# Where the sums of the experts are added to the output, and up to which step expert work is dealt out

## The chip, the cores and the metric

The kernel runs on one core of a Trainium2 chip. The metric is the device time of one execution in microseconds (us); less is better. Three runs of the kernel before gave 1726.62, 1738.76 and 1740.42 us, with a median of 1738.76. A separate execution was taken with the hardware profiler.

## The reference, cut to what matters

Eight sequences (batches) of 512 tokens with 256 features go through two layers. The first is a two-directional state space block plus a mixture of experts. The second, which the change touches, is an attention block plus another mixture of experts, both on the same normalized input:

```
xn = layernorm(x)
x = x + attention(xn) + experts(xn)
```

The attention has 16 heads of 16 features and all 512 x 512 scores of a batch, which are scaled by a decay band before the softmax; its output goes through one more projection, Wo. The experts are seven two-matrix networks (256 to 1024 to 256, with relu) on at most 512 tokens each, chosen by the router's two largest weights, and an eighth that hands the token through with a weight. In the kernel that last weight is noop. An expert's results are added to the rows of the tokens that it was given, so one token's row can get sums from two experts.

## The kernel before, in words

The second layer is one loop of 128 steps: 8 batches by 4 groups of four heads (g) by 4 blocks of 128 keys (c). In step n, TensorE makes four score tiles of 128 x 512 (s_ps, L1576); VectorE multiplies each by the decay band and takes its maximum (L1579); ScalarE takes exponentials of the step before (L1593); TensorE multiplies those of the step before that with the values (o_ps, L1601). Four such products accumulate a group.

**A group's division.** divide() runs a little in each step after a group's last block. It writes the group's sums to HBM (od, L1693). After every second group it loads the row sums of eight heads (sm, L1703) and their numerators, turned, into one half of oT (L1708). VectorE inverts sm (L1711); SP writes the inverse out (rd, L1712) and loads it back spread over all rows (rb, L1714). VectorE multiplies oT by rb (L1717). Two halves make oT complete. oT has one buffer, so the first half of the next batch can only be loaded when the last reader of the one before is done. That reader is finish(): for each of four token blocks, TensorE multiplies by Wo (fin, L1536), ScalarE copies (fo), and VectorE adds noop times the token's own row (L1540), into x_sb, which has a place for all eight batches. The last batch goes another way, without HBM: its first eight heads are turned on chip by first_heads() (tq, tb), the last eight by Ending, which also projects and writes the output (L1530).

**The experts** are a generator of 238 turns, WORK. Two turns make one pair of the first matrix's columns or half of an output tile; each turn is about a microsecond of TensorE. In each step, fill() takes up to two turns and a third one if the work is behind its due time, which grows evenly from step 4 to step LAST. A turn can end with an expert output half done; then nothing else is dealt out before the next turn. Each expert output tile (e_yo) is added row by row into x1 in HBM by a scatter that GpSimd issues (L1437). x1 holds the layer's input x. Each of these scatters waits for the landing of the one before.

**soon()** runs one part of what stands first in the list urgent: finish() or first_heads(). It is called once a step ahead of the turns, and does nothing while an expert output is half done. When all turns are spent, fill() calls it as well, up to three times a step in all.

**combine()** starts when all turns are spent. It adds x1 into x_sb, batch by batch, by accumulating DMAs that GpSimd issues (L1548), the last batch first, and then writes seven batches from x_sb to the output (L1557). The last batch is written by Ending.

Order matters as follows. The engines take their instructions strictly in program order, and so does each queue of DMAs. SP's queue carries the loads of queries, keys and values (qT, kT, vt), the expert weights (e_w, 1 MB each) and all DMAs of divide(). GpSimd's queue (q0) carries the gathers and scatters of the experts and the accumulating DMAs. At the end of the program a flag is loaded by all engines (L1880) and a branch is taken; only behind that does GpSimd wait for its DMAs to land.

Of the kernel before, what the change touches and what calls it, by code (L numbers as in the profile page):

```python
# [12 lines left out]
ALU = mybir.AluOpType  # L13
# [5 lines left out]
B, S, DM = 8, 512, 256  # L19
NT = B * S  # L20
NTILE = NT // P
TPB = S // P
# [36 lines left out]
def bc(ap, axis, shape):  # L59

    return ap.unsqueeze(axis).to_broadcast(shape)
# [3 lines left out]
def tile_kernel(ctx: ExitStack, tc: tile.TileContext, t, out: bass.AP):  # L65
    nc = tc.nc
    V, A, G, T, Y = nc.vector, nc.scalar, nc.gpsimd, nc.tensor, nc.sync
# [46 lines left out]
    x1 = dram.tile([NT, DM], FP, name="x1", tag="x1")  # L114
# [7 lines left out]
    def rows_of(src, b):  # L122
        return src[b * S : (b + 1) * S, :].rearrange("(c p) d -> p c d", p=P)
# [248 lines left out]
    def bank(name, shape, tag="gen"):  # L372
        return mp.tile(shape, FP, name=name, tag=("e", "s")[tag] if isinstance(tag, int) else tag, bufs=2)
# [6 lines left out]
    def rows_in():  # L380
# [29 lines left out]
        for u, b0 in zip(us, order[::2]):  # L410
# [9 lines left out]
            nm = r0p.tile([P, G2], FP, name="nm", tag="nm")  # L420
            V.scalar_tensor_tensor(nm, mv[:, :, 0], -1.0, rs, ALU.mult, ALU.mult)
            finish(1)
            for i in range(G2):
                A.activation(
# [3 lines left out]
            for k, b in enumerate(both):  # L428
# [5 lines left out]
                for o in range(KC):  # L434
# [7 lines left out]
                    else:  # L442
                        A.copy(xTs[b][:, o, :], tp)
            turned.append((both, halves))
        finish(2)
        return xTs

# [120 lines left out]
    with ExitStack() as es:  # L568
# [26 lines left out]
        held = {}  # L595
# [770 lines left out]
    x_sb = res.tile([P, NTILE, DM], FP, name="x_sb", tag="x_sb")  # L1366
    with tc.tile_pool(name="a1", bufs=1) as p1, tc.tile_pool(name="a2", bufs=2) as p2, tc.tile_pool(
# [109 lines left out]
        def columns(tq):  # L1477

            tq = tq.rearrange("p g (i r) -> p (g i) r", r=32)
            V.tensor_tensor(low[:, :8], low[:, :8], tq[:, :, AD], ALU.min)  # L1480
            sm = p2.tile([P, 8], FP, name="smq", tag="smq")
            V.reciprocal(sm, tq[:, :, AD])
            oq = p2.tile([P, 8, AD], FP, name="oq", tag="oq")
            V.tensor_tensor(oq, tq[:, :, :AD], bc(sm, 2, [P, 8, AD]), ALU.mult)
            return oq.rearrange("p h d -> p (h d)")

        def first_heads(oT, os):

            for c in range(TPB):
                at = slice(c * P, (c + 1) * P)  # L1490
                tq = bank("tq", [P, 2, P])
                for k in range(2):
                    T.transpose(tq[:, k, :], os[k][:, at], ident)
                oq = columns(tq)
                yield
                yield
                tp = bank("tb", [P, P])
                T.transpose(tp, oq, ident)
                A.copy(oT[:, 0, at], tp)
                yield  # L1500

        class Ending:
# [11 lines left out]
            def divide(self):  # L1514
                tq = psum.tile([P, 2, P], FP, name="tq", tag="s_ps", bufs=4)
                T.transpose(tq[:, 0, :], self.os[:, self.at], ident)
                T.transpose(tq[:, 1, :], self.last, ident)
                self.oq = columns(tq)
# [13 lines left out]
        def finish(b, oT):  # L1532
            for c in range(TPB):
                fp = bank("fin", [P, DM])
                for j in range(KC):
                    T.matmul(fp, oT[:, j, c * P : (c + 1) * P], w_o[:, j, :], start=(j == 0), stop=(j == KC - 1))  # L1536
                fo = p2.tile([P, DM], FP, name="fo", tag="fo")
                A.copy(fo, fp)  # L1538
                xi = x_sb[:, b * TPB + c, :]
                V.scalar_tensor_tensor(xi, xi, noop[:, b * TPB + c : b * TPB + c + 1], fo, ALU.mult, ALU.add)  # L1540
                yield
            finished.add(b)

        def combine():


            def add(b):
                G.dma_start(out=x_sb[:, b * TPB : (b + 1) * TPB, :], in_=rows_of(x1, b), accum_op=ALU.add)  # L1548

            for b in (B - 1, *range(B - 2)):  # L1550
                add(b)
            yield
            while B - 2 not in finished:
                yield
            add(B - 2)
            for b in range(B - 1):
                G.dma_start(out=rows_of(out, b), in_=x_sb[:, b * TPB : (b + 1) * TPB, :])  # L1557

        class Step:
            def __init__(self, b, g, c, inputs):
# [117 lines left out]
        def divide(b, g, op, od, rd, held):  # L1680


            if b == B - 1:
                if g == 0:
                    held.append(p1.tile([P, KC, S], FP, name="oT", tag="oT"))
                held.append(p1.tile([P, S], FP, name="ol", tag="ol", bufs=3))
                A.copy(held[-1], op)
                if g == 1:
                    urgent.insert(0, first_heads(held[0], held[1:]))
                return  # L1690
            os = p1.tile([P, S], FP, name="os", tag="row", bufs=2)
            A.copy(os, op)
            Y.dma_start(out=od[g].rearrange("i r s -> (i r) s"), in_=os)  # L1693
            yield
            if g % 2 == 0:
                return
            j = g // 2
            if j == 0:
                held.append(p1.tile([P, KC, S], FP, name="oT", tag="oT"))
            oT = held[0]  # L1700
            sm = p2.tile([P, 32], FP, name="sm", tag="sm")
            for gg in range(2):
                Y.dma_start(  # L1703
                    out=sm[64 * gg : 64 * gg + 64, :],
                    in_=od[2 * j + gg, :, AD, :].rearrange("i (p f) -> i p f", f=32),
                )
            for gg in range(2):
                Y.dma_start(out=oT[64 * gg : 64 * gg + 64, j, :], in_=od[2 * j + gg, :, :AD, :])  # L1708
            yield
            V.tensor_tensor(low, low, sm, ALU.min)  # L1710
            V.reciprocal(sm, sm)  # L1711
            Y.dma_start(out=rd[8 * j : 8 * j + 8, :].rearrange("h (p f) -> (h p) f", f=32), in_=sm)  # L1712
            rb = p1.tile([P, S], FP, name="rb", tag="row", bufs=2)
            Y.dma_start(out=rb, in_=bc(rd[8 * j : 8 * j + 8, :], 1, [8, AD, S]))  # L1714
            yield
            yield
            V.tensor_tensor(oT[:, j, :], oT[:, j, :], rb, ALU.mult)  # L1717
            yield
            if g == 3:
                urgent.insert(0, finish(b, oT))  # L1720

        with tc.manual_schedule(engines=ENGINES):
# [15 lines left out]
            finished = set()  # L1738
            urgent, idle, chains = [], [], []
            WORK = NE1 * 2 * (1 + FC + 2 * 4)  # L1740
            LAST = 118
            spent = 0

            def due():

                return WORK * (n - 4) / (LAST - 4)

            rows, number1 = combine(), None
            e1, e2 = given()
            work = experts()  # L1750
# [44 lines left out]
            for n in range(N + 2):  # L1795

                if n < N:
                    b, g, c = steps[n]
# [40 lines left out]
                if m >= 0:  # L1839
                    s = done[m]  # L1840
                    if s.c == 0:
                        s_op = psum.tile([P, S], FP, name="o_ps", tag="o_ps", bufs=2)
                    s.values(s_op)
                    if s.c == TPB - 1:
                        if m == N - 1:
                            tails = [Ending(s.b, c, s_op, s.scratch[2]) for c in range(TPB)]
                        else:
                            chains.append(divide(s.b, s.g, s_op, *s.scratch))
                            next(chains[-1], None)
# [87 lines left out]
def build(arrays):  # L1937
    import concourse.bacc as bacc

    nc = bacc.Bacc("TRN2", target_bir_lowering=False, num_devices=1)  # L1940
    t = {
        k: nc.dram_tensor(f"in_{k}_dram", v.shape, mybir.dt.from_np(v.dtype), kind="ExternalInput").ap()
        for k, v in arrays.items()
    }
    out = nc.dram_tensor("out_0_dram", (NT, DM), FP, kind="ExternalOutput").ap()
    with tile.TileContext(nc) as tc:
        tile_kernel(tc, t, out)
    return nc
# [10 lines left out]
```

## Time and profile before

| what | us |
|---|---|
| time of the profiled execution | 1731.81 |
| its span | 1730.0 |
| TensorE busy | 1571.1 (91%) |
| VectorE busy | 1172.8 (68%) |
| ScalarE busy | 917.1 (53%) |
| GpSimd busy | 573.1 (33%) |
| attention loop, steps 0 to 127 | about 1170 to 1710 |
| eight accumulating DMAs, issue of the first | 1669.83 |
| last computation (L1879) | 1723.33 |

The chain of work that ended last is TensorE for 73% of the span and VectorE for 17%. Granted clock means the share of full speed that TensorE's clock had. In lists by order of time the first two columns are the start and the duration in us, then come engine, line, operation, output and inputs, and in brackets how long the engine stood idle before and for what. SPq and POOLq are the queues that issue DMAs; "x6" is a count, and the duration of a group reaches from its first start to its last end. A matmul in fp32 stands in the trace as several records, so "x8" are four score tiles or two turns of expert work. Windows list, for each stretch, the busy time of each engine with its count, then granted clock, DMA share and GB/s.

### The profile page before, as it was taken

Reading aid. Unit: us, or ns where it says so; the run is one execution under the profiler, and the core shown is the slowest. Engines: PE = TensorE matmul, PEld = TensorE weight load, DVE = VectorE, ACT = ScalarE, POOL = GpSimd, SP = SyncE. Lnnn points to the kernel's source line nnn. Section 1 sums busy time; section 2 is a strip of 40 time slices with the busy share of each in tenths; the row PEclk is TensorE's granted clock in tenths of the full one; section 3 lists DMA queues with packets and bytes.
Section 4 is the critical chain, followed back from the end, with each engine's and each line's share of the span. In section 5 each row is a group of like instructions: output and inputs, shape, how many; then the busy total and the mean of one; then the engine's idle time right before and its main releaser. Section 6 shows DMA issues by size and latency. Waiting matters only on the chain.

```text
span 1730.0 us, 25735 instructions
## 1 busy us (share of the span) xinstructions
PE 1571.1 (91%) x8700; PEld 963.3 (56%) x8700; DVE 1172.8 (68%) x3067; ACT 917.1 (53%) x2173; POOL 573.1 (33%) x518
## 2 busy tenths in 40 slices
PE   6556799989999999999789898889999999999996
PEld 6324467767777677677445555644445445444442
DVE  6577775576576665775786836547777777777674
ACT  4222345445354454454455643137777777777773
POOL 0031556556564465564532421010111111112030
PEclk7676899999999999999989899669999999999996
DMA  8010346455554564464355624133423343334254
GB/s 298 18 55 0 137 151 221 156 178 177 173 194 157 164 212 158 160 219 159 83 118 166 184 86 136 50 122 118 137 81 107 101 134 102 88 113 136 71 89 134
DMA packets 131821, 231.09 MB, mean 134 GB/s; under 512 B 20109, under 2 KB 93839, under 8 KB 120528
## 3 DMA queue, kind: packets, MB, share of 16 engines
q1 hardware_dynamic: 101952, 119.46, 22.0%
q0 software_dynamic: 28656, 108.69, 20.7%
q8 instruction: 73, 1.20, 0.3%
q10 hardware_dynamic: 1072, 1.18, 0.2%
q14 instruction: 68, 0.56, 0.1%
HBM read 176.75 MB, written 53.58 MB: 133 GB/s over the span
## 4 chain that ended last, share of the span: by engine, by line
PE 73%; DVE 17%; ACT 4%; DMA 3%; issue 2%; POOL 0%; SPq 0%; ACTq 0%; DVEq 0%; POOLq 0%
PE pj L943 8%; PE s_ps L1576 7%; PE o_ps L1601 7%; PE h_ps L640 7%; PE y_ps L664 7%; PE e_hp L1419 5%; PE e_yp L1432 5%; PE op L1088 3%; PE yd L1169 3%; DVE cv L956 3%; PE seg L1131 3%; PE sp L1199 2%; ACT s L1593 2%; PE yoff L1187 2%; DVE s L1579 2%
## 5 line engine op out<-in xcount | busy, mean ns | idle before, releaser
L1579 DVE CUSTOM_DVE_ANT_0 s<-s_ps,band 128x512 f32<-128x512 f32 x512 | 323.3, 687 | 142.5 <-PE s_ps L1576 138.4
L1593 ACT ACTIVATE s<-s,ng 128x512 f32<-128x512 f32 x512 | 325.7, 708 | 0.0
L943 PE MATMUL pj<-xT,w_w_in 128*128 128x512 f32 x384 | 198.1, 642 | 8.9 <-DVE cv L956 6.6
L1437 POOL DMA_INDIRECT x<-e_yo,number x28 | 45.0, 1606 | 432.6 <-ACT e_yo L1436 386.2
L1576 PE MATMUL s_ps<-qT,kT 16*128 16x512 f32 x1024 | 166.4, 671 | 4.4 <-DMA qT<-qd 4.4
L956 DVE SCALAR_TENSOR_TENSOR cv<-pj,w_conv_w,cv 128x511 f32<-128x511 f32 (+2 forms) x192 | 143.4, 747 | 21.9 <-ACT cv L952 17.4
L1115 POOL TENSOR_TENSOR au<-da,half 128x512 f32<-128x512 f32 x64 | 77.9, 1217 | 228.1 <-PE seg L1131 153.1
L640 PEld LDWEIGHTS h_ps<-xdT,w 128*128 128x128 f32 x1152 | 138.1, 193 | 19.3 <-issue 18.6
L1601 PE MATMUL o_ps<-s,wv 128*32 128x512 f32 x1024 | 144.3, 636 | 1.2 <-ACT w L1589 1.2
L640 PE MATMUL h_ps<-xdT,w 128*128 128x128 f32 x1152 | 141.4, 276 | 0.7 <-DMA w<-in_w_dram,w_idx 0.7
L664 PE MATMUL y_ps<-w,hT 128*128 128x256 f32 x576 | 138.7, 385 | 0.0
L664 PEld LDWEIGHTS y_ps<-w,hT 128*128 128x128 f32 x576 | 108.3, 193 | 30.0 <-issue 16.1
L943 PEld LDWEIGHTS pj<-xT,w_w_in 128*128 128x128 f32 x384 | 70.1, 200 | 90.8 <-issue 78.8
L1576 PEld LDWEIGHTS s_ps<-qT,kT 16*128 16x128 f32 x1024 | 51.6, 190 | 120.5 <-DVE w L1586 41.9
L1432 PE MATMUL e_yp<-e_w,e_hT 128*128 128x256 f32 x448 | 114.0, 392 | 1.4 <-ACT e_yo L1436 0.9
L1419 PE MATMUL e_hp<-e_xdT,e_w 128*128 128x256 f32 x448 | 111.9, 388 | 3.5 <-ACT fo L1538 2.2
L1178 DVE TENSOR_TENSOR yT<-yT,yd 128x512 f32<-128x512 f32 (+1 forms) x64 | 43.8, 684 | 104.8 <-PE yd L1169 103.8
L1144 ACT ACTIVATE mt<-seg,mid 64x64 f32<-64x64 f32 x512 | 109.4, 309 | 0.8
L1432 PEld LDWEIGHTS e_yp<-e_w,e_hT 128*128 128x128 f32 x448 | 79.9, 189 | 52.3 <-issue 31.9
L1419 PEld LDWEIGHTS e_hp<-e_xdT,e_w 128*128 128x128 f32 x448 | 81.9, 190 | 39.4 <-ACT s L1593 15.4
L960 ACT ACTIVATE th<-cv 128x512 f32<-128x512 f32 x64 | 40.3, 630 | 116.1 <-DVE cv L956 108.8
L952 ACT ACTIVATE cv<-pj,w_conv_b,w_conv_w 128x512 f32<-128x512 f32 x64 | 49.8, 778 | 95.1 <-PE pj L943 91.0
(341 smaller groups left out, 2827.3 us busy)
## 6 DMA issues: line engine op xcount, KB each, us to landing
ex<-exd SPq DMA_DIRECT2D x96, 128.0 KB
fr<-fdd SPq DMA_DIRECT2D x64, 128.0 KB
e_w<-in_ei_dram SPq DMA_DIRECT2D x7, 1024.0 KB
e_w<-in_eo_dram SPq DMA_DIRECT2D x7, 1024.0 KB
od<-os SPq DMA_DIRECT2D x28, 256.0 KB
vd<-vt SPq DMA_DIRECT2D x16, 272.0 KB
vt<-vd SPq DMA_DIRECT2D x8, 544.0 KB
u<-in_u_dram SPq DMA_DIRECT2D x8, 512.0 KB
```

The source lines that it names most:

```text
L640: T.matmul(hp[:, i, :], w1[:, k * FF + f * P : k * FF + (f + 1) * P], xdT[:, k * P : (k + 1) * P], start=(k == 0), stop=(k == KC - 1),)
L664: T.matmul(yp, hT[f // 4][:, f % 4, :], w2[:, f * DM : (f + 1) * DM], start=(f == 0), stop=(f == FC - 1),)
L943: T.matmul(pj, w_in[:, k, o * P : (o + 1) * P], self.xT[:, k, :], start=(k == 0), stop=(k == KC - 1))
L956: V.scalar_tensor_tensor(cv[:, s:], pj[:, : S - s], conv_w[:, q, 3 - s : 4 - s], cv[:, s:], ALU.mult, ALU.add)
L1115: G.tensor_tensor(self.au, bc(da[:, d, self.i, :], 2, HH), bc(TRI[d], 1, HH), ALU.mult)
L1144: A.activation(mt[lo, over, h], seg[lo, over, h], AF.Exp, bias=mid[lo, self.i, h : h + 1])
L1419: T.matmul(hp, w1[:, k, f * P : (f + 1) * P], xdT[:, k, :], start=(k == 0), stop=(k == KC - 1))
L1432: T.matmul(yp, hT[:, f, c * P : (c + 1) * P], w2[:, f, :], start=(f == 0), stop=(f == FC - 1))
L1576: T.matmul(sp[i], self.k[r, cols], self.q[r, :], start=True, stop=True)
L1579: V.tensor_tensor_reduce(out=self.p[i], in0=sp[i], in1=band[:, at : at + S], scale=1.0, scalar=KEEP, op0=ALU.mult, op1=ALU.max, accum_out= ...
L1593: A.activation(self.p[i], self.p[i], AF.Exp, bias=self.ng[:, i : i + 1])
L1601: T.matmul(op[32 * i : 32 * i + 32, :], self.wv[:, i, :], self.p[i], start=(self.c == 0), stop=(self.c == TPB - 1),)
```

## The change

A batch that is finished is written to the output at once, by SP. Behind the experts the last batch is still added into x_sb; for the seven others x1 is added to the output in HBM, where both the source and the destination lie in HBM. So the seven additions into x_sb and the seven writes by GpSimd are gone, and there are seven writes by SP and seven accumulating DMAs into the output. Each of the latter waits for its batch's write. first_heads() goes to the end of the list urgent, not to its front. LAST is 124, not 118.

```diff
@@ finish(b, oT)
+            Y.dma_start(out=rows_of(out, b), in_=x_sb[:, b * TPB : (b + 1) * TPB, :])
             finished.add(b)
 
         def combine():
-            def add(b):
-                G.dma_start(out=x_sb[:, b * TPB : (b + 1) * TPB, :], in_=rows_of(x1, b), accum_op=ALU.add)
-            for b in (B - 1, *range(B - 2)):
-                add(b)
-            yield
-            while B - 2 not in finished:
-                yield
-            add(B - 2)
-            for b in range(B - 1):
-                G.dma_start(out=rows_of(out, b), in_=x_sb[:, b * TPB : (b + 1) * TPB, :])
+            b = B - 1
+            G.dma_start(out=x_sb[:, b * TPB : (b + 1) * TPB, :], in_=rows_of(x1, b), accum_op=ALU.add)
+            for b in range(B - 1):
+                while b not in finished:
+                    yield
+                G.dma_start(out=rows_of(out, b), in_=rows_of(x1, b), accum_op=ALU.add)
@@ divide
                 if g == 1:
-                    urgent.insert(0, first_heads(held[0], held[1:]))
+                    urgent.append(first_heads(held[0], held[1:]))
@@ the loop's constants
-            LAST = 118
+            LAST = 124
```

Batches and steps are counted from 0. The order in which the changed program's instructions stand on each engine is known without a run.

## The prediction

> **What bounds the kernel now.** I read the stages first (busy time in windows of 50 us), then the chain of waits, then TensorE, SP, DVE and GpSimd in order of time. From 1170 us to the end runs the attention loop of 128 steps. A step with two turns of expert work is the sum of its TensorE work: s_ps 1.07 + expert 1.93 + o_ps 1.00 = 4.00 us in the chain; DVE needs about 3.0 us of it and waits. So the loop is TensorE's, until the experts end in step 118:
>
> ```profile
> 1661.41 1.14 PE L1576 MATMUL s_ps<-qT,kT 16*128 16x512 f32 x8
> 1665.40 1.53 PE L1576 MATMUL s_ps<-qT,kT 16*128 16x512 f32 x8
> ...
> 1684.62 2.09 PE L1576 MATMUL s_ps<-qT,kT 16*128 16x512 f32 x8
> ...
> 1689.34 1.19 PE L1576 MATMUL s_ps<-qT,kT 16*128 16x512 f32 x8
> 1704.82 2.09 PE L1576 MATMUL s_ps<-qT,kT 16*128 16x512 f32 x8
> ```
>
> These are the starts of steps 118, 119, 123, 124 and 127. Behind 119 nothing fills TensorE; transposes of the last batch wait for DVE (first line below, 2.24 us idle), and then the granted clock (third number from the right) falls to a half, as the windows say:
>
> ```profile
> 1682.26 0.33 PE L1498 MATMUL tb<-ident,oq 128*128 128x128 f32 x1 [2.24 <-DVE oq L1484]
> 1680.00:1682.00 2.00, 0.03 (x1) 0.00 (x0) 1.93 (x11) 1.67 (x3) 1.15 (x2) 1.00 1.22 186
> 1684.00:1686.00 2.00, 2.00 (x12) 0.52 (x8) 0.00 (x0) 1.44 (x3) 0.75 (x1) 0.50 1.25 196
> ```
>
> Beside this tail run the accumulating DMAs (GpSimd in order of time):
>
> ```profile
> 1665.39 1.55 POOL L1437 DMA_INDIRECT x<-e_yo,number  x1 [6.57 <-ACT e_yo L1436]
> 1669.83 10.53 POOL L1548 DMA_DIRECT2D x_sb<-x  x8 [2.89 <-DVE x_sb L1540]
> 1679.47 1.68 POOL L1557 DMA_DIRECT2D out_dram<-x_sb  x1
> 1696.01 0.75 POOL L1557 DMA_DIRECT2D out_dram<-x_sb  x1 [1.90 <-DMA x_sb<-x]
> ```
>
> Eight sums of 512 KB move from 1672 to 1693.5, 2.69 us each at 195 GB/s; the writes end at 1703.5. The last computation, L1879, starts at 1723.33; flag load, branch and barrier take the rest to 1730.0. GpSimd waits there for its DMAs at 1724.5, with about 1 us to spare, since TensorE comes to the barrier later: DMAs that land by 1725.5 cost nothing now.
>
> The third place is the single oT buffer, in SP's and DVE's order of time for batch 6:
>
> ```profile
> 1616.44 1.07 SPq L1708 DMA_DIRECT2D oT<-od  x2
> 1617.56 3.28 SPq L1466 DMA_DIRECT2D kT<-kd  x6
> 1621.38 0.34 SPq L1712 DMA_DIRECT2D rd<-sm  x1
> 1623.06 0.61 SPq L1714 DMA_DIRECT2D rb<-rd  x1
> 1629.20 0.68 DVE L1717 TENSOR_TENSOR oT<-oT,rb 128x512 f32<-128x512 f32 x1
> 1351.65 0.69 DVE L1717 TENSOR_TENSOR oT<-oT,rb 128x512 f32<-128x512 f32 x1 [1.97 <-DMA rb<-rd]
> ```
>
> The last line (batch 2) shows that this chain is short of time already: DVE waited 1.97 us for rb. Four of fourteen such products waited, 5.8 us in all.
>
> **1. Dealing to step 124.** The number of expert turns stays the same; in the changed program's instruction order the seven steps with three turns become two-turn steps, and the last turns stand in step 123. Up to step 124 TensorE has, beyond what it had done before step 119, five more bare steps, 5 x 2.07 = 10.35 us, and the four projections of batch 6 (fin, 1.06 us each, now in steps 118 to 122), 4.24 us. 1665.40 + 14.6 = 1680.0, against 1689.34: -9.35 us. That holds if TensorE stays the bound: its sums give 68.5 us a batch, 69.4 are measured.
>
> **2. The tail.** Appending first_heads puts its transposes into steps 124 to 127, where they were in 122 to 124. A transpose (tb) that stands in the same step as its DVE columns stalls the step: before, 6.89 us (step 122) and 6.92 (124); others took 4.72, 3.88, 4.68. Now 124 and 125 stall and 126 does not: 6.3 (like 122, with one pair of transposes less and half of it at full clock) + 6.92 + 4.72 = 17.95 us up to step 127, where 1704.82 - 1689.34 = 15.48 were: +2.5. From step 127 to the end I keep 25.2 us. Parts 1 and 2 make -6.85. Bounds: at full clock (o_ps 1.00 and s_ps 1.07 for 1.87 and 2.06) the three steps are 5.7 + 6.1 + 3.5 = 15.3 us and the end some 2 shorter, -11.5 in all; with 8.0 for step 125 and 6.9 for 124, about -5.
>
> **3. What the slower pace does to oT.** finish() runs one projection at a call of soon(), and none while an expert output is half done. At the new pace more calls fall on half-done outputs: the last fin of batches 3, 4 and 5 moves from steps 74, 90, 106 to 76, 92, 108, the thirteenth of the next batch. oT has one buffer, so L1708 of that batch waits for it, and SP's queue stands: six kT loads (not needed for some steps), then rd and rb, for which DVE waits in L1717 one step on; DVE's own place for L1717 has not moved. With T the start of step 108: fin ends T + 2.13; two oT issues 1.07 and six kT 3.28 make T + 6.5 for rd; rb goes 2.64 us behind (median of the seven such pairs, 1.68 to 3.05), T + 9.1; where DVE waited, rb landed 4.28 to 4.62 us after its issue: T + 13.5. L1717 is due 3.87 us into the next step (1629.20 - 1625.33), which begins at T + 5.06: T + 8.9. DVE stalls 4.6 us; in a quiet step its fourth read of s_ps ends at 1653.12 and the next s_ps (from 1653.42) needs that bank at about 1654.2, a slack of 1.1 us, so TensorE loses 3.5 us, three times: **+10.5**. Lower bound 0 (both landings like the shortest in such a chain, 1.41 us: T + 9.3); upper, with 3.05 and 4.62 and, in batch 5, a 1 MB weight load ahead on SP (2.7 us at the 390 GB/s of the plain writes), about +15. I take the middle because its rows are the same transfers in the same order.
>
> A TensorE gap of about 2 us also comes with each of these waits. The row shows a clock falling after 2.2 us idle, and half clock from 1682.7 to 1689.3, 3.3 us lost; the 1.97 us DVE wait at 1351 left it at 1.00 for its whole 50 us window. I take 0, and keep +3.3 each for the range. [...]
>
> **4. The outputs.** Seven SP writes replace seven GpSimd writes: 0.34 us of SP's issue each, waiting for the DVE result of the last fin. Behind them in SP's queue stand od writes and loads due two or more steps on: 0, at most +2 together if rb queues behind 512 KB (1.3 us).
> Of the eight sums only x_sb of the last batch stays into SBUF and goes first; it is read some 22 us later, so it is hidden. Seven are HBM to HBM, which no row shows. Nearest are the sums into SBUF, 2.69 us for 512 KB, and the scatter-adds into HBM, 128 KB in 1.2 to 1.4 us from first to last packet, where the middle 0.3 us also runs at 184 to 205 GB/s. So 2.69, and 4 x 1.4 = 5.6 as the other end. Before, DMA traffic began 10.6 us behind the start of the last expert step; now that step starts at 1676 + 10.5 = 1686.5, traffic 1697.1, the first sum lands 1699.8, seven more 1718.6. The cover reaches 1725.5 + 3.65 = 1729.2: price **0**, up to 4.2 us a sum; at 5.6 it is 1739.0, +9.8. GpSimd's later wait blocks nothing else.
> [...]
>
> **Sum.** -6.85 + 10.5 = +3.65 us on the profiled execution's 1731.81 (span 1730.0 and 1.81 around it): **1735.5**. The median of the runs shown is 1738.76, of 1726.62 to 1740.42, so executions spread by -5 to +9 about the profiled one.
>
> **The rivals.**
> A, the oT waits are absorbed (rb lands in 1.4 to 2 us): 1725.0, with the clock up in the tail 1720.3. For it: ten of the fourteen products found rb landed. Against: every landing that a wait measures took over 4.2 us, and rd now starts 7 us later than in the rows above. 0.25.
> B, the clock falls at each oT wait: +10, 1745.4. For it the 2.2 us row, against it 1351. 0.15.
> C, slower: the HBM-to-HBM sums take over the end. One price decides, that of a sum; from 4.2 us on it counts, and the time is 1699.8 + 7 x price + 4.5 + 1.81: 1745.3 at 5.6, above 1% at 6.2, 1751.6 at 6.5. [...] 0.15.
> D, nothing moves where I say (the pace does not change the order): excluded, the order is known. The forecast keeps 0.45.
>
> 1% of the median, 17 us, is about what a measurement of this kernel can tell from no change. Forecast, A and half of B and C lie within it: same 0.70. Slower by more: the upper half of C, B joined to long waits, 0.20. Faster by more needs A at full clock and a low draw of the spread: 0.10. The range goes from A at 1722 to the lower part of C, 1752.
>
> **What would show it.** s_ps of step 124 starts 9 us earlier less the waits before it (about 1690); L1717 of batches 4, 5, 6 waits 4 to 6 us for rb, and s_ps two steps on comes 3 to 4 us late; TensorE at half clock from step 124 or 125; q0 traffic from about 1697 to 1719. L1717 without waits makes A, a clock below 1 in steps 78, 94, 110 makes B, q0 traffic beyond 1729 makes C. I am wrong altogether if the 2.07 us of bare steps or the stalls of the last transposes do not hold.

## The result, and the profile after

The changed kernel takes 1759.48 us (median of four executions, 1752.63 to 1761.59); beside it the kernel before takes 1737.24 us. The ratio is 1.0121, 95% interval 1.0072 to 1.0171: slower by about 1.2%, and outside the predicted range of 1722 to 1752. The profiled execution took 1757.68 us, span 1755.8. One execution of e6 below took 1866.47 us at a mean granted clock of 0.81, where all others had 0.91 to 0.94; the ratios leave it out.

TensorE in order of time, as before (start, duration, instruction, idle time ahead of it):

```profile
1679.09 1.14 PE L1569 MATMUL s_ps<-qT,kT 16*128 16x512 f32 x8
...
1707.27 1.14 PE L1569 MATMUL s_ps<-qT,kT 16*128 16x512 f32 x8
...
1711.89 0.30 PE L1498 MATMUL tb<-ident,oq 128*128 128x128 f32 x1 [3.11 <-DVE wv L1590]
1712.12 1.79 PE L1594 MATMUL o_ps<-s,wv 128*32 128x512 f32 x8
1713.84 2.09 PE L1569 MATMUL s_ps<-qT,kT 16*128 16x512 f32 x8
...
1719.41 0.45 PE L1498 MATMUL tb<-ident,oq 128*128 128x128 f32 x1 [2.86 <-DVE oq L1484]
...
1722.08 2.09 PE L1569 MATMUL s_ps<-qT,kT 16*128 16x512 f32 x8
...
1726.80 2.09 PE L1569 MATMUL s_ps<-qT,kT 16*128 16x512 f32 x8
```

The s_ps lines are steps 118, 124, 125, 126 and 127. Step 124 starts at 1707.27, 17.9 us later than before, where about 1690 was forecast; step 118 is 17.7 us late already. So most of the loss lies ahead of the tail. The two tb lines are the stalls of steps 124 and 125.

The third place of the profile before, SP's queue and DVE's product by rb, here in batch 4, with DMAs of batch 5 and the products of batches 5 and 6 behind it:

```profile
1480.18 1.07 SPq L1701 DMA_DIRECT2D oT<-od  x2
1481.30 2.77 SPq L1466 DMA_DIRECT2D kT<-kd  x6
1484.30 0.34 SPq L1705 DMA_DIRECT2D rd<-sm  x1
1487.03 0.61 SPq L1707 DMA_DIRECT2D rb<-rd  x1
1491.48 0.69 DVE L1710 TENSOR_TENSOR oT<-oT,rb 128x512 f32<-128x512 f32 x1 [4.71 <-DMA rb<-rd]
1492.46 1.06 PE L1594 MATMUL o_ps<-s,wv 128*32 128x512 f32 x8 [2.60 <-DVE wv L1590]
...
1554.21 1.07 SPq L1701 DMA_DIRECT2D oT<-od  x2
1555.33 0.46 SPq L1414 DMA_DIRECT2D e_w<-in_eo_dram  x1
1560.54 0.34 SPq L1705 DMA_DIRECT2D rd<-sm  x1
1565.23 0.61 SPq L1707 DMA_DIRECT2D rb<-rd  x1
...
1569.87 0.69 DVE L1710 TENSOR_TENSOR oT<-oT,rb 128x512 f32<-128x512 f32 x1 [9.06 <-issue]
1570.85 1.94 PE L1594 MATMUL o_ps<-s,wv 128*32 128x512 f32 x8 [5.75 <-DVE wv L1590]
...
1645.42 0.69 DVE L1710 TENSOR_TENSOR oT<-oT,rb 128x512 f32<-128x512 f32 x1 [5.24 <-DMA rb<-rd]
1646.40 1.07 PE L1594 MATMUL o_ps<-s,wv 128*32 128x512 f32 x8 [3.13 <-DVE wv L1590]
```

DVE stands 4.71, 9.06 and 5.24 us in front of rb; behind it stands wv, and for wv TensorE stands 2.60, 5.75 and 3.13 us. For the second of these waits the profile names no releaser ("issue" in the row); that it is rb there too is read from its issue, which lies 4.64 us ahead of the product (4.45 and 4.18 us in batches 4 and 6). That chain was forecast, in these three batches. What was not is in the windows around the third of them (length, then busy time of TensorE, weight load, DVE, ScalarE, GpSimd; third from the right TensorE's granted clock, then DMA share and GB/s):

```profile
1644.00:1646.00 2.00, 0.00 (x0) 0.00 (x0) 0.58 (x1) 0.02 (x1) 0.00 (x0) 1.00 1.02 342
1646.00:1648.00 2.00, 1.60 (x10) 0.79 (x12) 2.00 (x7) 0.00 (x0) 0.00 (x0) 0.87 0.93 249
1648.00:1650.00 2.00, 2.00 (x8) 1.02 (x5) 1.61 (x8) 0.99 (x3) 0.00 (x0) 0.50 0.23 42
1652.00:1654.00 2.00, 2.00 (x6) 1.46 (x5) 0.64 (x4) 1.13 (x4) 0.00 (x0) 0.50 0.20 78
```

Each gap is followed by 6.8 to 10.2 us at half clock. The pairs of steps around the three waits (78 and 79, 94 and 95, 110 and 111) took 14.35, 19.20 and 15.20 us for the 7.98 us of two quiet steps: 24.8 us more.

GpSimd and the same view of the end:

```profile
1711.55 1.39 POOL L1548 DMA_DIRECT2D x_sb<-x  x1 [2.87 <-DVE smq L1482]
1712.36 9.52 POOL L1552 DMA_DIRECT2D out_dram<-x  x7
```

```profile
1714.00:1715.00 1.00, 1.00 (x8) 0.35 (x8) 0.00 (x0) 1.00 (x2) 1.00 (x4) 0.50 1.02 125
...
1734.00:1735.00 1.00, 1.00 (x7) 0.20 (x3) 0.00 (x0) 0.41 (x1) 0.00 (x0) 0.50 1.24 199
1735.00:1736.00 1.00, 1.00 (x5) 0.00 (x0) 0.00 (x0) 0.00 (x0) 0.00 (x0) 0.50 1.03 163
```

One sum into SBUF and seven within HBM, 4.2 MB, move from 1714.1 to 1735.8: 2.7 us each, the rate of the sums into SBUF before (2.69 us). The last computation (L1872) starts at 1747.42, so they are hidden.

Where the 25.9 us between the two profiled executions went, from step 7 of the loop, whose start differs by 1.3 us:

| stretch | before | after | difference |
|---|---|---|---|
| step 7 to step 124 | 507.7 | 526.9 | +19.2 |
| step 124 to 127 | 15.48 | 19.53 | +4.05 |
| step 127 to the last computation | 18.5 | 20.6 | +2.1 |
| last computation to the end of the span | 6.7 | 8.4 | +1.7 |

### The profile page after: what moved, and what is told of

Same layout as the page of the kernel before. It is cut to its first block, busy times and chain, and to the rows that moved or that the text cites. A ratio compares the mean times of both kernels' runs of the same rounds, so it can differ in the third digit from the quotient of the medians.

```text
span 1755.8 us, 25758 instructions
## 1 busy us (share of the span) xinstructions
PE 1575.5 (90%) x8700; PEld 963.3 (55%) x8700; DVE 1178.3 (67%) x3067; ACT 917.7 (52%) x2173; POOL 567.5 (32%) x511
## 5 line engine op out<-in xcount | busy, mean ns | idle before, releaser
L640 PEld LDWEIGHTS h_ps<-xdT,w 128*128 128x128 f32 x1152 | 139.9, 195 | 19.3 <-issue 18.5
```

What stands on the lines that cost most here:

```text
L640: T.matmul(hp[:, i, :], w1[:, k * FF + f * P : k * FF + (f + 1) * P], xdT[:, k * P : (k + 1) * P], start=(k == 0), stop=(k == KC - 1),)
```

## The experiments

Executions differ in when the loop's step 7 begins (between 1172 and 1200 us in the profiled runs below, though what lies ahead of the loop is the same code), so besides the median each profile is read from the start of step 7 to the start of the last computation ("loop"). Before it is 541.7 us, after 567.0.

| run | median us | ratio to before | loop us |
|---|---|---|---|
| e1 three halves of oT | 1735.80 | 0.999 [0.9954, 1.0027] | 545.0 |
| e2 pace alone | 1756.21 | 1.0123 [1.0071, 1.0175] | 565.5 |
| e3 outputs alone | 1740.19 | 1.0018 [0.9992, 1.0044] | 547.8 |
| e4 loads behind | 1754.67 | 1.0104 [1.0070, 1.0138] | 559.9 |
| e5 filler | 1754.32 | 1.0114 [1.0057, 1.0170] | 555.7 |
| e6 product two steps later | 1735.94 | 0.9997 [0.9972, 1.0022] | 542.4 |
| e7 tail in turn | 1747.96 | 1.0067 [1.0044, 1.0091] | 559.3 |
| e8 = e6 + e7 | 1727.02 | 0.9947 [0.9922, 0.9972] | 535.4 |
| e9 = e1 + e6 + e7 | 1725.49 | 0.9934 [0.9909, 0.9959] | 524.0 |
| e10 = e9 at step 118 | 1723.66 | 0.9902 [0.9872, 0.9932] | 531.5 |
| e11 = e9, tail filled | 1730.65 | 0.9956 [0.9934, 0.9979] | 531.9 |
| e12 rd ahead of the loads | 1751.40 | 1.0072 [1.0045, 1.0099] | 554.9 |
| e13 = e10 again | 1725.90 | 0.9928 [0.9901, 0.9956] | 531.6 |
| e14 = e9 at step 121 | 1723.19 | 0.9920 [0.9889, 0.9952] | 526.8 |
| e15 = e9 again | 1726.50 | 0.9927 [0.9898, 0.9957] | 525.2 |
| e16 before, tail in turn | 1728.26 | 0.9932 [0.9904, 0.9960] | 530.3 |

**The theory** is that the pace makes the last projections late, the single oT buffer makes SP, rb and DVE late, and TensorE's clock falls in the gap. **Rivals**: the new outputs cost it; the denser expert work slows the loads.

**e1: no wait for the buffer.**

```diff
-            if j == 0:
-                held.append(p1.tile([P, KC, S], FP, name="oT", tag="oT"))
-            oT = held[0]
+            held.append(p1.tile([P, S], FP, name="oT", tag="oT", bufs=3))
+            oT = held[j]
```

(and the users of oT take the half j; to make room the fall-back branch, which does not run here, loads its rows in quarters.)

> oT is held as two halves of 512 columns out of three buffers, so that the load of the next batch's first half finds a free one and does not wait for the last projection. Theory (the wait for the single oT buffer, and the clock that falls behind it): the three pairs of steps at 1486.8, 1560.8 and 1640.2 that took 14.35, 19.20 and 15.20 us go back to 2 x 3.99 = 7.98 us each, 24.8 us less: about 1757.7 - 24.8 = 1733 (ratio to the kernel before 0.99 to 1.00), DVE waits at the product by rb of 2 us or less in batches 4, 5 and 6, TensorE's clock 1.00 there. Rival 1 (the new outputs cost it): unchanged, 1757. Rival 2 (the denser expert work itself slows the loads): rb still comes late, over 1750.

Measured: 1735.80, 22 us back in the loop. Batches 4 and 6 have no wait at the product any more. In batch 5 DVE still waits 4.32 us: as in the changed kernel, a 1 MB expert weight stands right behind the oT load, and rd and rb come behind it; the clock falls there for 6.8 us. Batch 1 keeps a wait of 3.30 us. So the theory holds for batches 4 and 6 in full, and in batch 5 for about half of the wait.

**e2 and e3: the two halves of the change apart.** e2 is the kernel before with

```diff
-                    urgent.insert(0, first_heads(held[0], held[1:]))
+                    urgent.append(first_heads(held[0], held[1:]))
...
-            LAST = 118
+            LAST = 124
```

> The kernel before with the experts dealt to step 124 and first_heads appended, its outputs left as they were (sums into SBUF, then seven writes by GpSimd). Theory (pace alone makes the loss): about as slow as the changed kernel, 1757; at most 5 us more if the seven writes behind the sums end last (sums 1714 to 1736, then 7 x 1.4 us: 1746, about when the last computation starts). Rival 1 (the outputs cost it): about 1737.

and e3 has the diff's other part (finish() writes, combine() adds in memory) without these lines.

> The kernel before with the new outputs alone (SP writes each finished batch, GpSimd adds the experts' sums in memory), dealing to step 118 and the order of first_heads as before. Theory: no change, 1732 to 1741 (ratio 0.998 to 1.002); the sums take 2.69 us each as into SBUF. Rival 1: 1750 or more.

e2 reproduces the whole loss: ratio 1.0123 for 1.0121, with waits at rb of 4.54, 9.02 and 5.33 us in batches 4, 5 and 6. e3's interval holds 1. Its profile, though, shows a cost that the median does not settle. SP in batch 3, and DVE's product:

```profile
1414.29 1.07 SPq L1701 DMA_DIRECT2D oT<-od  x2
1415.46 0.41 SPq L1542 DMA_DIRECT2D out_dram<-x_sb  x1
1415.92 4.12 SPq L1466 DMA_DIRECT2D kT<-kd  x6
1420.20 0.34 SPq L1705 DMA_DIRECT2D rd<-sm  x1
1423.35 0.61 SPq L1707 DMA_DIRECT2D rb<-rd  x1
...
1427.91 0.69 DVE L1710 TENSOR_TENSOR oT<-oT,rb 128x512 f32<-128x512 f32 x1 [4.73 <-DMA rb<-rd]
```

The same place in the kernel before:

```profile
1410.04 1.07 SPq L1708 DMA_DIRECT2D oT<-od  x2
1411.16 2.77 SPq L1466 DMA_DIRECT2D kT<-kd  x6
...
1420.90 0.69 DVE L1717 TENSOR_TENSOR oT<-oT,rb 128x512 f32<-128x512 f32 x1 [1.67 <-DMA rb<-rd]
```

The 512 KB write L1542 stands between oT and the loads; the six loads take 4.12 us of issue where they took 2.77, and DVE waits 4.73 us where it waited 1.67. The clock fell here as well, for 3.4 us; the two steps (62 and 63) took 13.43 us where the same two took 9.81. In the changed kernel the same order stands in batch 1, with a wait of 3.40 us and two steps of 12.11 (e2, without the write, waited 1.53 there, and the two took 8.59). So one of the seven SP writes cost about 3.5 us in each of these two executions; for the others no step up to 123 shows a cost above 0.6 us.

**e4 and e12: rd and rb ahead of the loads.** e4 moved load_some(6) behind the chains in every step; e12 only in the step that issues rd and rb:

```diff
-                load_some(6)
+                if n % 16 != 11:
+                    load_some(6)
                 for chain in list(chains):
                     if next(chain, "end") == "end":
                         chains.remove(chain)
+                if n % 16 == 11:
+                    load_some(6)
```

> The changed kernel with the step's six q and k loads issued behind the chains' DMAs instead of ahead of them: rd and rb no longer queue behind six kT loads on SP; the oT buffer is still one. Theory: rb comes 2.8 to 3.7 us sooner, DVE's waits of 4.71, 9.06 and 5.24 us become about 1.9, 5.4 and 2.5; TensorE gets back 2.3 + 3.7 + 2.8 us and, where its gap falls under 2 us (batches 4 and 6), 3.3 us of half clock each: 15.4 us less, 1742; 1739 if batch 5 keeps its clock too. If only the wait for the buffer counts and the loads between do not: 1757.

> The changed kernel, one oT buffer, with the six kT loads of the step in which rd and rb are issued (the twelfth of a batch) moved behind them, the six of the step before left ahead of oT: what e4 meant to try and did not, since there another step's six loads came between. If the loads between oT and rd make the wait long: rd 2.8 us sooner, DVE's waits 4.71, 9.06 and 5.24 become about 1.9, 5.4 and 2.4, TensorE's gap falls under 2 us in batches 4 and 6 and the clock stays: 1742 to 1745. If not: 1755 to 1759.

e4 is no test of this: the six loads of the step before moved too, to between oT and rd, so rd came no sooner (4.49 us behind the oT issue in batch 4, where it was 4.12), and its waits of 4.92, 8.48 and 4.78 us say nothing of the loads. e12 has rd 1.24 us behind oT in batch 4, and waits of 3.67, 6.48 and 3.36 us: 12.1 us back in the loop, 8 in the median (ratio 1.0072 for 1.0121, with intervals that overlap). Less than expected, since rb, which waits for rd to land, was issued 4.3 to 7.1 us behind rd instead of 2.7 to 4.7. The loads were part of the delay, the late oT load the larger part.

**e5: does the clock fall because TensorE is idle?** Three matmuls that nobody reads, ahead of o_ps in the steps of the gaps:

```diff
+                if n in (78, 94, 110):
+                    idle_bank = bank("fill", [P, S])
+                    for _ in range(3):
+                        T.matmul(idle_bank, ident, band[:, :S], start=True, stop=True)
                 m = n - 2
```

> The changed kernel with three more matmuls (128x512, a constant tile by a constant tile, never read) on TensorE ahead of o_ps in steps 78, 94 and 110, where it stood idle for 2.60, 5.75 and 3.13 us; by fin (1.06 us for 512 columns) they take 3.2 us. DVE's waits for rb stay. Theory (the clock falls because TensorE stands idle): in batches 4 and 6 the clock stays 1.00 and 3.3 us come back in each, in batch 5 some 2.5 us of idle time are left: 1757.7 - 6 = 1752, or 1749 if batch 5 keeps its clock too. Rival (the clock falls for another reason, the burst of work behind the wait): the half clock stays and the matmuls only cost, 1758 to 1767.

Windows of e5 around batch 6, to be held against the four of the changed kernel above:

```profile
1644.00:1646.00 2.00, 1.97 (x5) 1.01 (x6) 0.38 (x1) 0.26 (x1) 0.00 (x0) 1.00 1.03 316
1646.00:1648.00 2.00, 2.00 (x13) 0.40 (x13) 2.00 (x7) 0.00 (x0) 0.00 (x0) 1.00 0.90 346
1648.00:1650.00 2.00, 2.00 (x9) 0.69 (x7) 1.97 (x10) 0.80 (x3) 0.00 (x0) 1.00 0.17 38
```

DVE waits as long as before (TensorE's idle time of 3.13 us is filled), and the clock stays 1.00, in batch 4 as well; in batch 5 a half clock of 3.4 us is left of 10.2. The three pairs of steps took 2.3, 2.1 and 2.7 us less; the loop 11.3, since behind step 127 the clock came back sooner too (17.3 us for 20.6). Useless work made the kernel faster in the profiled execution; the median, 1754.3, is 5 us under the changed kernel's, but against the kernel before the ratio is 1.0114 for 1.0121. That the idle time makes the fall is shown by the clock rows (1.00 from 1648 to 1650, where the changed kernel has 0.50); a gain in the whole time is not shown.

**e6: DVE's product two steps later**, nothing else moved:

```diff
             yield
             yield
+            for _ in range(2 if j == 0 else 0):
+                yield
             V.tensor_tensor(oT[:, j, :], oT[:, j, :], rb, ALU.mult)
```

> The changed kernel with the product of oT's first half by rb two steps later in DVE's order (some 8 us); the single oT buffer and SP's order stay. Theory (the loss is DVE standing in front of rb, no transfer being needed earlier): no wait at this product, the three pairs of steps back at 7.98 us and the pair of batch 1 (12.1 us) too: 1757.7 - 24.8 - 4.1 = 1729, under the version with three halves of oT by its batch-5 and batch-1 waits. Rival (SP's queue is what is late: kT, the loads of the next batch): s_ps or the loads then wait in its place, 1745 or more.

Measured: 1735.94, the loop 24.6 us shorter, no wait over 1.22 us at any product. SP still stands at the oT load, but nobody stands behind it, until batch 6, where an expert weight is what comes late (TensorE of e8, which has the same place):

```profile
1625.76 1.13 PE L1419 MATMUL e_hp<-e_xdT,e_w 128*128 128x256 f32 x4
1629.96 2.05 PE L1432 MATMUL e_yp<-e_w,e_hT 128*128 128x256 f32 x4 [3.07 <-DMA e_w<-in_eo_dram]
```

The step and the next took 9.11 and 6.3 us for 7.98: a wait moved, and with it 7.4 us of the gain. So the rival was right for one batch in three.

**e7 and e8: the tail.** In first_heads each tb went out in the step of its own columns; now one step behind:

```diff
                 oq = columns(tq)
-                yield
-                yield
+                for _ in range(4):
+                    yield
                 tp = bank("tb", [P, P])
                 T.transpose(tp, oq, ident)
                 A.copy(oT[:, 0, at], tp)
-                yield
```

> The changed kernel with each back transpose tb of first_heads one step behind its columns instead of in the same step (one c a step in steps 124 to 127, the last tb in 128). Theory of the tail (tb waits for DVE columns emitted in its own step): steps 124, 125 and 126 go from 6.57 + 8.24 + 4.72 = 19.5 us to about 4 us each, 7.5 us less, 1750; if TensorE then keeps its full clock, some 4 us more, 1746. Rival (the bare tail is slow of itself, by the half clock): 1757.

> The two edits together (product two steps later, tb one step behind its columns). Theory: the gains add, 1757.7 - 28.9 - 7.5 to 11.5 = 1717 to 1721, faster than the kernel before by about 1% (ratio 0.988 to 0.992). If the outputs or the experts' sums then end last: not under 1724.

e7: 1747.96, 11.5 us under the changed kernel. e8: 1727.02, where 1717 to 1721 were expected; the 7.4 us above are lost in e6 as well as in e8. In the loops the two gains add to within 1 us: 24.6 and 7.7 us apart, 31.6 together.

**e9 to e11.** e9 joins e1, e6 and e7, e10 deals the same kernel to step 118, e11 adds one unread matmul to each of steps 124 to 127.

> The changed kernel with three halves of oT, the first half's product two steps later, and tb one step behind its columns. In the version with the last two edits alone (median 1727.0) SP still stood at the oT load; there TensorE waited 3.07 us for an expert weight that had queued behind it, and the clock fell: two steps of 9.11 + 6.30 us for 7.98, 7.4 us in all. Theory: these go too, 1727.0 - 7.4 = 1719.6 (ratio 0.988 to 0.992). Rival (that weight load is late of itself): 1727.

> The same kernel with the experts dealt to step 118: what the dealing is worth once its waits are gone. By part 1 of the prediction (-9.35 us for the dealing): about 1719.6 + 9 = 1729. If six more steps under expert work are worth nothing: the same as at 124, 1720.

> The same kernel (124) with one more matmul of 512 columns, never read, in each of steps 124 to 127 (1.06 us at full clock). Theory (in the tail too the clock falls because TensorE has too little to do beside DVE): it stays 1.00 to step 127, steps of 4.71 us become about 3.9, and the o_ps behind them take 1.0 for 1.9 us: 3 us less than without, 1716 to 1717. Rival: the matmuls only cost, 4 us more.

e9's loop is 524.0 us, 11.4 under e8's, and has no half clock at all between step 7 and the last computation; but its median of 1725.49 is only 1.5 us under e8's and stays 6 us over the expectation. e10 was against the theory: at 118 the median is no worse than at 124. e11's median is 5 us above e9's, but it tests nothing of the clock: e9 has no half clock in its tail to win back, and in e11 the unread matmul (fill) itself waited in steps 125 and 126 for ScalarE's copy of tb, since it takes a bank from the two that tq and tb use:

```profile
1682.93 1.69 PE L1832 MATMUL fill<-band,ident 128*128 128x512 f32 x2 [1.51 <-ACT oT L1499]
1689.88 1.82 PE L1832 MATMUL fill<-band,ident 128*128 128x512 f32 x2 [1.70 <-ACT oT L1499]
```

Those two steps took 7.04 and 7.08 us for 3.84 and 3.36 in e9, and the clock fell in both.

**e13 to e16: is the dealing worth anything by itself?** The kernel of e9 dealt to 118, 121 and 124 side by side, and the kernel before with e7's edit alone.

> e10 once more, beside 121 and 124 on the same chip. If the dealing by itself is worth its 9 us (part 1 of the prediction): about 1733, ratio 0.996 or more, and slower than 124 by some 0.5%. If the dealing is worth nothing: the same as 124 within 0.2%.

> The same kernel dealt to step 121. If each step of dealing is worth 1.5 us: between the other two, about 1729. If the dealing is worth nothing: the same as both.

> e9 once more, for the comparison with 118 and 121: 1723 to 1727, ratio to the kernel before 0.991 to 0.996.

> The kernel before, with each tb one step behind its columns and nothing else (dealing to 118, outputs and waits for oT as before). Before, steps 122 and 124 took 6.89 and 6.92 us, 123, 125 and 126 took 4.72, 3.88 and 4.68. If the tail's order is what e13 gains: 2 x 2.2 us less and some half clock, about 1731, ratio 0.995 to 0.997; if the edits around oT are: no change, 0.999 to 1.001.

The times put all four within 0.3% of each other, 0.992 to 0.9932 of the kernel before, each with an interval of 0.3% to either side. The loops say 531.6, 526.8, 525.2 and 530.3 us, so 6.4 us lie between 124 and 118, and 7.4 between e9 and e10. Some of it is clock: in e10 and e13 it is at a half through steps 122 and 123, which take 5.3 and 4.7 us, where e16, dealt to 118 as well, takes 3.2 and 3.1 at the full clock. Whether the dealing is worth those 6 to 7 us in the whole time stays open: the medians don't show them, the profiled executions do, and I have no reading of why. What is settled is the tail: on the kernel before, its order alone is worth 0.7% (0.4 to 1.0). e16, TensorE in steps 123 to 126:

```profile
1686.92 1.65 PE L1575 MATMUL s_ps<-qT,kT 16*128 16x512 f32 x8
...
1689.98 1.96 PE L1575 MATMUL s_ps<-qT,kT 16*128 16x512 f32 x8
1691.87 0.33 PE L1498 MATMUL tb<-ident,oq 128*128 128x128 f32 x1
1692.04 0.38 PE L1493 MATMUL tq<-ident,ol 128*128 128x128 f32 x2
1692.35 1.07 PE L1600 MATMUL o_ps<-s,wv 128*32 128x512 f32 x8
1693.34 1.96 PE L1575 MATMUL s_ps<-qT,kT 16*128 16x512 f32 x8
...
1696.70 1.97 PE L1575 MATMUL s_ps<-qT,kT 16*128 16x512 f32 x8
```

Steps of 3.1 to 3.4 us, no idle time ahead of tb, o_ps at 1.07 us, the full clock. DVE is the bound there: in windows of the same stretch it is busy for 1.93 to 2.00 us of 2, and four score tiles take 1.96 us at the clock at which they take 1.14 beside expert work. e8 to e11 and e13 to e16 beat both kernels; the simplest of them is e16, which takes three lines out and puts two in.

## Why the prediction was wrong

- **Part 1, the dealing (-9.35 us to the start of step 124): right in size** once the waits are gone. From step 7 to step 124 e9 and e15 take 496.8 and 497.9 us, before 507.7: -10.9 and -9.8. Of this, 4.6 us are the stalls of the last transposes, which lay ahead of step 124 before: e16, dealt to 118 with the tail in turn, takes 503.1. The dealing alone is worth the other 5 to 6 us there. In the changed kernel itself part 3's waits hide it: 526.9.
- **Part 2, the tail (+2.5 up to step 127, nothing behind): mis-sized.** It measured 4.05 and 3.8. Step 125 took 8.24 us, where the row of step 124 before (6.92) was taken and 8.0 was the bound: all of it runs at half clock now. Behind step 127 the half clock lasts to 1736.2 and comes again from 1739.6 to 1743.0, finq takes 5.30 us, and 1.7 us lie behind the last computation. "I keep 25.2 us" was a choice without a row for it.
- **Part 3, the oT waits (+10.5): this is the step that failed, by its second half.** Mechanism, batches, order of the transfers and even DVE's waits in batches 4 and 6 (4.71 and 5.24 for 4.6 us) were right; in batch 4 rd, rb and the product stand 6.4, 9.1 and 13.5 us behind the start of step 76, where 6.5, 9.1 and 13.5 were forecast. Batch 5, with the weight load that the prediction put into its upper bound, waited 9.06. But "I take 0" for the clock, with the 2.2 us row against it, was the wrong choice of two: it fell at all three waits, for 6.8, 10.2 and 6.8 us. Half of that time, without the 1.9 us of it in which TensorE stood idle anyway, is 11.0 us, an estimate that takes all of the rest as bound by TensorE (e5 got 7.1 back, with 3.4 us of half clock and its own matmuls left in); the other 13.8 of 24.8 are then the waits themselves, inside the bounds of 0 and 15. The row of 1351 that argued for 0 was a DVE wait of 1.97 us, not a TensorE gap of that length: TensorE was busy for 49.41 us of that window's 50.
- **Part 4, the outputs (0): right for the sums, wrong for one write.** 2.7 us a sum, hidden, traffic beginning 10.8 us behind the start of the last expert step (10.6 forecast). Of the SP writes the prediction said at most +2; in batch 1 it was about 3.5, clock included.
- **The sum**: -10 (part 1) + 24.8 (part 3) + 4 (batch 1, of which some 3.5 by the write) + 4 + 3.8 (part 2) = +26.6, less 1.3 us of an earlier start, is 25.3, against 25.9 measured. Rival B was the right rival (0.15) with too low a price: it had 1745.4, since it kept the 10.5 us and the tail. The chances went wrong in one place: the clock was treated as a coin beside the waits, when in the runs it fell with the long waits and hardly ever with the short ones. In the eighteen profiled executions 24 DVE waits at this product lasted 3.3 us or more, and the clock fell during 22 of them or within 6.3 us behind (the other two are filled ones of e5); of the 31 waits of 0.3 to 2.73 us this holds for two. The two belong in one case.

## What to carry to other kernels

Price a wait that leaves TensorE idle as two terms, the wait and the half clock behind it, and let the second grow with the first: here DVE waits of 4.71, 9.06 and 5.24 us had 6.8, 10.2 and 6.8 us of half clock behind them, and 13.8 us of waiting cost an estimated 11.0 more. When a change slows the pace of one queue of work, follow every buffer that this work frees; the cheapest remedy was not another buffer but moving the one instruction that stood in line to two steps later (e6). And look at what a loop's last steps do before dealing work into them: a transposition issued one step behind its inputs (e16) gave 0.7%, some 11 us, where the change had been forecast to win 9 by its dealing.

## What the runs showed of the hardware

In the two profiled executions of the kernels before and after, each of the 51 and 61 changes of TensorE's granted clock lies a whole multiple of 3.413 us behind the first, to within 0.003 us. Falls (to a half) and rises (to 1.00) in the changed kernel, from step 78 to the first rise in its tail:

| clock | at us | stretches of 3.413 us since the last |
|---|---|---|
| falls | 1493.88 | |
| rises | 1500.71 | 2.00 |
| falls | 1568.97 | 20.00 |
| rises | 1579.21 | 3.00 |
| falls | 1647.48 | 20.00 |
| rises | 1654.30 | 2.00 |
| falls | 1712.33 | 17.00 |
| rises | 1736.22 | 7.00 |

From step 7 on the same holds for all changes in the eighteen profiled executions, each with its own offset. The idle time of TensorE within one such stretch was held against them. The three falls at the waits came behind 1.99, 3.41 and 2.34 us of it, one in e5 behind 1.69, and up to the last computation no stretch at full clock with more than 1.64 us (e9) kept the clock. Falls came behind less as well: of the 46 up to there 22 came behind stretches with more than 1.64 us and 24 behind stretches with less. In the changed kernel one came behind 0.85 us (1739.64) and one behind a stretch that the profile shows busy throughout (1285.67), in e12 one behind 0.51, while stretches with up to 1.51 us here kept the clock. So no amount of idle time divides the two in these executions, and what else counts stays open. At the third wait TensorE is idle from 1643.3 to 1646.4, and half clock begins at 1647.48, the end of the stretch from 1644.07: some 4 us behind the start of the gap, when TensorE is at work again.
